# Splitting the copied columns 62 to 66 between ScalarE and VectorE, and copying 108 groups at other rates

## The chip, the cores and the metric

The kernel runs on one core of a Trainium2 chip. The metric is the time of one execution on the device in microseconds (us); the median of several runs is given. The engines are named as the profile names them: PE (TensorE, matmul) and PEld (its weight loads), DVE (VectorE), ACT (ScalarE), POOL (GpSimd), SP (SyncE, which issues DMAs).

## The reference

One layer of message passing on a graph of 12500 nodes with 64 features and 200000 edges with 32 features. The edges come sorted by destination.

```
msg_in    = concat(nodes[src], nodes[dst], edge_features)        # 200000 x 160
messages  = relu(msg_in @ mW1 + mb1) @ mW2 + mb2                 # 160 -> 128 -> 64
agg       = segment_sum(messages, dst, 12500)
upd       = relu(concat(nodes, agg) @ uW1 + ub1) @ uW2 + ub2
out       = layernorm(nodes + upd)
```

## The kernel before

The product of the source node's features with its rows of mW1 is computed once per node: a table `tab_a` of 12500 rows of 128 numbers, in device memory, and likewise `tab_b` for the destinations. Then the edges are worked off in 261 groups of 6 tiles of 128 edges (the last group has 3 tiles), one group to a step `s` of a long unrolled loop. For a group:

- POOL gathers the source rows of `tab_a` with one indirect DMA per tile (L223, into `xg`). It may run up to some nine groups ahead; a group's buffer comes free when its rows have been added.
- PE (`edge_part(s)`, L385) multiplies the edges' features and a one-hot selection of the destination's rows into a PSUM tile `pc`. It is issued one step ahead.
- DVE (`node_part(s)`, L408) adds the gathered rows to `pc`; ACT (L409) takes the ReLU into `h`.
- PE (`collect(s)`, L441 and L444) sums `h` by destination, one step later. The messages' second layer is applied after the sum.
- About every ten steps at first, and every four at the end, a stretch of nodes is complete and is updated, normalised and stored (`close`, `update`, `activated`, `residual`, `squares`, `statistics`, `deviation`, `norm`, `store`).

Some groups are **copied groups** (the list `COPIED`). Of such a group, POOL gathers 4 tiles instead of 6. For the other two tiles the features of the source nodes are copied, one column of 128 numbers per pair of edges (one edge of each tile), out of a transposed copy of the nodes that lies on chip (`xtop` has the features in the upper half of its partitions and zeros below, `xbot` the other way round). A copy adds or ORs a column of the one and a column of the other into a column of `xc`. A copied group has 128 such columns. PE then multiplies `xc` by the weights (L388, four matmuls of a copied group, with accumulation into `pc`).

The columns are shared out by `ACTS`: columns 0 to ACTS - 1 of a copied group are copied by ACT (`singly`, an ACTIVATE with the other column as bias, L358), the rest by DVE (`joined`, a bitwise OR, L365). `portion(s, total)` gives the columns that are due in step `s`: `PACE` is a list of (first step, copied groups per step), `progress(s)` is its sum up to `s`, and of the j-th copied group the share `progress(s - 1) - j` to `progress(s) - j` is copied in step `s`. The j-th copied group is the one three steps after the step in which `progress` reaches j + 1, so that its columns are there when PE wants them; groups from 258 on are never copied.

The addresses of the columns are values in registers of the copying engine. `addresses` (L334) loads them with one register load for up to `CHUNK` = 8 columns of one copied group (two addresses a column).

`share` cuts a step's columns into parts, for the places where they are issued, and the parts into portions of up to 8 columns. DVE's columns of a step go into three parts in an even step and into two in an odd one, all parts but the last of a whole number of 8 columns. DVE's order in an even step: add (L408), first part, comparison of the next 12 tiles' destinations (`select`, L257), second part, `sel` (L263), last part. In an odd step: add, first part, last part. Work of the updates stands between. ACT's columns of a step are issued at its end, in one part (`singly(s, 0, 1)`): ReLU, work of the updates, all the columns, next ReLU.

Of the kernel before, what the change touches and what calls it, by code (L numbers as in the profile page):

```python
# [70 lines left out]
U8 = mybir.dt.uint8  # L71
YBASE = XBASE + 4 * XCOLS
LEAD = 8
PACE = ((11, 0.435), (50, 0.458), (130, 0.438), (170, 0.425), (261, 0))
FINAL = 258


def progress(s):

    return sum(r * max(0, min(s + 1, b) - a) for (a, r), (b, _) in zip(PACE, PACE[1:]))  # L80

# [3 lines left out]
    while progress(s) >= len(COPIED) + 1 and s + 3 < FINAL:  # L85
        COPIED.append(s + 3)
LAST = 4 * (N - 1)
ACTS, CHUNK = 64, 8


def updates():
# [934 lines left out]
```

## Time and profile before

| | |
|---|---|
| median of 3 runs | 1726.23 us (1725.64 to 1727.5) |
| the profiled execution | 1724.81 us, its span 1723.0 us |
| mean granted clock of TensorE | 0.582 |
| busy: PE, DVE, ACT, POOL | 84%, 62%, 90%, 74% of the span |
| gathers (L223) | 1289 from `tab_a`, 60 from `in_x` |
| column copies | 6848 on ACT (L358), 6848 on DVE (L365) |
| register loads for them (L334) | 1006 on ACT, 1037 on DVE |

The profile is of one execution. Busy time counts what an engine's datapath does; the load of a register or the issue of a DMA is not counted. "Idle before" is the time in which an engine did nothing ahead of an instruction, with what ended it; "issue" means that nothing in the profile held it up, which includes the engine's own sequencer loading registers or preparing a DMA.

### The profile page before, as it was taken

The numbers are of one execution on the slowest core, as the hardware profiler recorded it, in microseconds if no ns is written. First come the engines' busy times: TensorE is split into PE (matmuls) and PEld (weight loads), VectorE is DVE, ScalarE is ACT, GpSimd is POOL, SyncE is SP. The second block draws the span as 40 slices with busy tenths as digits, with TensorE's granted clock in tenths as the row PEclk, the third lists the DMA queues.
The fourth block names the chain that finished last, engine by engine and source line by source line (L and its number), as shares of the span: only waits on it lengthen the run. The fifth ranks groups of instructions, "written<-read, shape, count | busy, mean of one in ns | idle before, by whom it ended". The sixth has DMA issues, their size and how long they took to land. (4 is left out here: it accounts for less than half of the span.)

```text
span 1723.0 us, 47177 instructions
## 1 busy us (share of the span) xinstructions
PE 1444.9 (84%) x9576; PEld 1251.9 (73%) x9608; DVE 1062.7 (62%) x7605; ACT 1555.2 (90%) x7279; POOL 1277.0 (74%) x1358
## 2 busy tenths in 40 slices
PE   2696888888878888888888988888887898999987
PEld 2585777787767777777776887776776677877776
DVE  1426666666666666666666666666666666666563
ACT  0176999999999999999999999999999999999892
POOL 7777777777777777777777777777777777777771
PEclk8575555556555555655565555556666656555576
DMA  8783433433333333333333333343333443334332
GB/s 208 202 182 99 118 109 111 125 101 93 94 95 97 92 101 94 98 102 96 105 98 108 108 109 106 104 112 110 108 104 107 112 111 109 110 107 111 105 108 63
DMA packets 205695, 190.92 MB, mean 111 GB/s; under 512 B 55938, under 2 KB 171862, under 8 KB 205414
## 3 DMA queue, kind: packets, MB, share of 16 engines
q1 hardware_dynamic: 147700, 92.42, 19.6%
q0 software_dynamic: 43168, 86.53, 18.4%
q10 hardware_dynamic: 14546, 8.93, 1.9%
q8 instruction: 91, 1.49, 0.3%
q14 instruction: 190, 1.55, 0.3%
HBM read 170.26 MB, written 17.47 MB: 109 GB/s over the span
## 5 line engine op out<-in xcount | busy, mean ns | idle before, releaser
L223 POOL DMA_INDIRECT xg<-tab_a,src_s x1289 | 1218.4, 945 | 393.1 <-issue 356.1
L358 ACT ACTIVATE xc<-xtop,xbot 128x1 f32 x6848 | 1299.2, 290 | 31.3 <-issue 21.4
L365 DVE TENSOR_TENSOR xc<-xtop,xbot 128x1 int32 x6848 | 584.7, 153 | 451.3 <-issue 440.2
L444 PE MATMUL sums<-sel,h 128*128 128x32 f32 x3126 | 642.9, 372 | 79.3 <-ACT h L409 78.4
L444 PEld LDWEIGHTS sums<-sel,h 128*128 128x128 f32 x3126 | 609.2, 296 | 104.4 <-ACT h L409 89.5
L385 PE MATMUL pc<-rhs,l 64*128 64x128 f32 x3126 | 421.0, 412 | 81.5 <-DVE tb L610 28.8
L385 PEld LDWEIGHTS pc<-rhs,l 64*128 64x128 f32 x3126 | 348.1, 289 | 145.4 <-issue 63.0
L408 DVE TENSOR_TENSOR pc<-pc,xg 128x768 f32<-128x768 f32 (+1 forms) x250 | 212.9, 852 | 76.9 <-PE pc L385 26.7
L409 ACT ACTIVATE h<-pc 128x768 f32<-128x768 f32 x250 | 200.3, 801 | 25.4 <-DVE pc L408 24.5
L257 DVE TENSOR_TENSOR l<-l,cps 128x768 f32<-128x768 int32 (+1 forms) x134 | 126.7, 945 | 28.9 <-DMA l<-in_dst_row 17.5
L441 PEld LDWEIGHTS <-one 128*1 128x1 bf16 x1563 | 57.6, 83 | 84.9 <-issue 74.8
L441 PE MATMUL cnt<-sel,one 128*1 128x32 bf16 x1563 | 94.3, 187 | 0.7 <-issue 0.5
L388 PE MATMUL pc<-w1a,xc 64*128 64x128 f32 x428 | 80.5, 384 | 0.0
L263 DVE TENSOR_TENSOR sel<-cps,drc 128x384 f32<-128x384 f32 x131 | 71.3, 545 | 12.6 <-PE sums L444 12.5
L223 POOL DMA_INDIRECT xg<-in_x,src_s x60 | 57.6, 959 | 19.1 <-issue 18.0
L388 PEld LDWEIGHTS pc<-w1a,xc 64*128 64x128 f32 x428 | 71.5, 298 | 0.0
L482 PE MATMUL pu<-xw,uz 128*128 128x480 f32 (+2 forms) x64 | 61.9, 1071 | 0.3 <-DVE xw L459 0.3
L602 ACT COPY tb<-pb 128x512 f32<-128x512 f32 (+1 forms) x13 | 7.4, 569 | 60.1 <-DMA tab_a<-tb 21.1
L439 PE MATMUL cnt<-zero_b 128*1 128x512 bf16 x32 | 18.5, 578 | 47.1 <-DVE xw L459 42.5
L483 PE MATMUL pu<-sums_s,w2u 128*128 128x480 f32 (+2 forms) x64 | 54.4, 952 | 0.0
L498 PE MATMUL cps<-ux,xw 128*128 128x64 f32 x244 | 45.7, 348 | 8.5 <-DVE sel L263 7.9
L498 PEld LDWEIGHTS cps<-ux,xw 128*128 128x128 f32 x244 | 41.0, 253 | 13.8 <-DVE sel L263 10.3
(111 smaller groups left out, 598.6 us busy)
## 6 DMA issues: line engine op xcount, KB each, us to landing
l<-in_dst_row SPq DMA_DIRECT2D x262, 96.0 KB
l<-in_eT SPq DMA_DIRECT2D x262, 96.0 KB
xg<-tab_a,src_s POOLq DMA_INDIRECT x1289
rhs<-tab_b SPq DMA_DIRECT2D x361, 32.0 KB
tab_b<-tb SPq DMA_DIRECT2D x13, 512.0 KB
rhs<-tab_b SPq DMA_DIRECT2D x387, 16.0 KB
tab_a<-tb ACTq DMA_DIRECT2D x12, 512.0 KB
out<-y SPq DMA_DIRECT2D x30, 128.0 KB
```

Of the source, the lines that this page charges most:

```text
L223: nc.gpsimd.indirect_dma_start(out=a[:, i, :] if s < XG else a[:, i // 2, i % 2, :], out_offset=None, in_=A[:, :] if s >= XG else x[:, :], ...
L257: nc.vector.tensor_tensor(l[r], l[r].bitcast(I32), node[r].unsqueeze(2).broadcast_to([r.stop - r.start, SUP // 2, P]), op=ALU.is_equal)
L263: nc.vector.tensor_tensor(s[:, :nt], slot.unsqueeze(1).broadcast_to([P, nt, WIN]), drc[:, g * SUP:g * SUP + nt].unsqueeze(2).broadcast_to( ...
L358: nc.scalar.activation(o[:, e:e + 1], top.bitcast(F32), AF.Identity, bias=bot.bitcast(F32))
L365: nc.vector.tensor_tensor(o[:, e:e + 1].bitcast(I32), top.bitcast(I32), bot.bitcast(I32), op=ALU.bitwise_or)
L385: nc.tensor.matmul(pc[:, b, k, :], L[g][q:q + 64, m, :], rhs[g % 2][q:q + 64, w, :], start=s >= XG or k == 0, stop=s >= XG and not copied)
L388: nc.tensor.matmul(pc[:, b, k, :], xc[s][q:q + 64], w1a[q:q + 64], start=False, stop=True)
L408: nc.vector.tensor_tensor(pc[:, :, :m], pc[:, :, :m], a[:, :, :m], op=ALU.add)
L409: nc.scalar.activation(h, pc, AF.Relu)
L441: nc.tensor.matmul(pn[:, bass.ds(ws[i], WIN)], one, SB[g][:, k0 + i, :, 1], start=False, stop=ends and i == n - 1)
L444: nc.tensor.matmul(ps[:, bass.ds(ws[i], WIN)], h[:, i % 2, i // 2, :], S[g][:, k0 + i, :], start=False, stop=ends and i == n - 1)
L498: nc.tensor.matmul(py[:, i], xw[u % 2][:, i * P:(i + 1) * P], ux, start=i == 0, stop=False)
```

## The change

ACT copies the first 62 columns of a copied group, DVE the other 66. The four rates of `PACE` rise by 2.6%, 2.2%, 0.6% and 0.7%; the list of copied groups that follows from them has 108 entries, not 107, and 75 of the 107 groups of before are replaced by a neighbour (one to four steps earlier for the same place in the list). Nothing else is changed.

```
-PACE = ((11, 0.435), (50, 0.458), (130, 0.438), (170, 0.425), (261, 0))
+PACE = ((11, 0.4465), (50, 0.468), (130, 0.4405), (170, 0.428), (261, 0))
...
-ACTS, CHUNK = 64, 8
+ACTS, CHUNK = 62, 8
```

## The prediction

> **What bounds the kernel now.** The page first: its span, and the busy share of each engine.
>
> ```profile
> span 1723.0 us, 47177 instructions
> PE 1444.9 (84%) x9576; PEld 1251.9 (73%) x9608; DVE 1062.7 (62%) x7605; ACT 1555.2 (90%) x7279; POOL 1277.0 (74%) x1358
> ```
>
> The groups name the work that the change touches: the gathers, and the copies on the two engines.
>
> ```profile
> L223 POOL DMA_INDIRECT xg<-tab_a,src_s x1289 | 1218.4, 945 | 393.1 <-issue 356.1
> L358 ACT ACTIVATE xc<-xtop,xbot 128x1 f32 x6848 | 1299.2, 290 | 31.3 <-issue 21.4
> L365 DVE TENSOR_TENSOR xc<-xtop,xbot 128x1 int32 x6848 | 584.7, 153 | 451.3 <-issue 440.2
> ```
>
> POOL's 74% is an artefact of what counts as busy: a gather takes 945 ns, and nearly all of the idle time before gathers is "issue" (393.1 / 1289 = 0.305 us each). So POOL gathers without a pause, every 1.25 us. It is not the bound, though. The timeline at the end shows how far ahead it is:
>
> ```profile
> 1688.95 0.94 POOL L223 DMA_INDIRECT xg<-tab_a,src_s  x1 [0.30 <-issue]
> ...
> 1703.06 0.97 DVE L408 TENSOR_TENSOR pc<-pc,xg 128x768 f32<-128x768 f32 x1
> ```
>
> The row at 1703.06 adds the rows of group 259. Those were gathered three gathers before the last one, so by 1688.95 - 3 x 1.25 + 0.94 = 1686.1: 17 us earlier. What uses the gathers is the late side, and the time is the sum of its steps. If it were never late, about 17 us could be had and no more.
>
> The busy time by stretch shows who holds up the steps. I cut the trace close to where the rate of the copies changes (steps 50, 130, 170) and at step 236, where the updates come about every fourth step; the second fence has the ReLUs, one to a step, of the first three stretches.
>
> ```profile
> core 0: us, PE busy (x) PEld busy (x) DVE busy (x) ACT busy (x) POOL busy (x), PEclk, DMA share, GB/s
> 121.00:384.00 263.00, 214.82 (x1451) 196.00 (x1451) 173.09 (x1206) 235.46 (x1112) 198.99 (x211) 0.51 0.40 111
> 384.00:890.00 506.00, 425.31 (x2725) 374.49 (x2730) 328.28 (x2531) 503.31 (x2457) 382.55 (x406) 0.54 0.34 97
> 890.00:1140.00 250.00, 222.92 (x1387) 192.91 (x1391) 163.62 (x1228) 246.74 (x1185) 189.03 (x201) 0.55 0.38 107
> 1140.00:1554.00 414.00, 360.78 (x2393) 303.66 (x2404) 271.22 (x1975) 402.83 (x1915) 312.77 (x332) 0.62 0.40 109
> 1554.00:1690.00 136.00, 121.96 (x784) 100.62 (x787) 82.06 (x566) 119.34 (x553) 102.94 (x109) 0.61 0.39 107
> ```
>
> ```profile
> L409 ACT ACTIVATE h<-pc x40: 782/788/811, 122.3 to 380.6; 128x768 f32<-128x768 f32 x40
> L409 ACT ACTIVATE h<-pc x80: 782/807/889, 387.0 to 886.1; 128x768 f32<-128x768 f32 x80
> L409 ACT ACTIVATE h<-pc x40: 783/792/810, 892.4 to 1135.7; 128x768 f32<-128x768 f32 x40
> ```
>
> Call the five stretches A to E. ACT is busy 99.5% of B and 98.7% of C. DVE seems to have a third of its time free, but that is the trap of this case. The waits, for A to E in order, say how much of the free time stands before a column copy with the cause "issue":
>
> ```profile
> DVE xc L365 <- issue: 65.7, 118, 1.6
> ...
> DVE xc L365 <- issue: 161.3, 309, 1.4
> ...
> DVE xc L365 <- issue: 71.8, 147, 1.1
> ...
> DVE xc L365 <- issue: 110.8, 222, 1.1
> ...
> DVE xc L365 <- issue: 30.7, 59, 1.0
> ```
>
> The timeline of one step in B, with ACT's copies of the same time, shows what that is:
>
> ```profile
> 707.43 0.51 DVE L365 TENSOR_TENSOR xc<-xtop,xbot 128x1 int32 x6 [0.56 <-issue]
> 707.86 0.69 DVE L408 TENSOR_TENSOR pc<-pc,xg 128x512 f32<-128x512 f32 x1
> 709.05 0.68 DVE L365 TENSOR_TENSOR xc<-xtop,xbot 128x1 int32 x8 [0.50 <-issue]
> 710.51 0.68 DVE L365 TENSOR_TENSOR xc<-xtop,xbot 128x1 int32 x8 [0.78 <-issue]
> ...
> 712.98 0.43 DVE L365 TENSOR_TENSOR xc<-xtop,xbot 128x1 int32 x4 [0.32 <-issue]
> 713.41 0.97 DVE L408 TENSOR_TENSOR pc<-pc,xg 128x768 f32<-128x768 f32 x1
> ```
>
> ```profile
> 709.78 5.30 ACT L358 ACTIVATE xc<-xtop,xbot 128x1 f32 x28 [0.23 <-issue]
> ```
>
> ```profile
> L334 DVEq TENSOR_LOAD <-col_a x1037: 342/1102/2403, 124.3 to 1679.9; - x173
> ```
>
> Before each portion of up to 8 columns the engine loads two addresses a column into registers. ACT hides that load behind its slow copies (28 in 5.30 us, 0.19 us each, no gap between); DVE copies 8 columns in 0.65 us and then stands still until the addresses are there. So its "issue" time is work, and DVE's occupation is busy plus issue: 489.6 of 506 us in B (96.8%), 235.4 of 250 in C, 382.0 of 414 in D, 112.8 of 136 in E, 238.8 of 263 in A. ACT and DVE are both nearly full. For ACT and DVE waiting on others in B I read:
>
> ```profile
> DVE pc L408 <- PE pc L388: 3.3, 3, 1.8
> DVE pc L408 <- PE pc L385: 2.8, 2, 1.9
> ...
> ACT h L409 <- DVE pc L408: 0.8, 2, 0.5
> ```
>
> Neither waits for the other to speak of: the bound is ACT by a hair, DVE is next.
>
> **The change, part by part.** Counting the lists of columns step by step, as the rates and the two shares give them, the copies of ACT change by -6, -24, -30, -42 and -50 in A to E, together -152 (6848 to 6696); those of DVE by +64, +126, +40, +70 and -20, together +280 (6848 to 7128). The last stretch loses on both because the last copied group is finished about a step and a half earlier.
>
> *ACT.* Each copy gone is 0.188 us (5.30 / 28): -1, -4.5, -5.6, -7.9 and -9.4 us, -28.6 in all. Its loads go from 1006 to 998 and are hidden either way.
>
> *DVE.* The number of loads hardly changes (1037 to 1038); they become wider, because the added columns nearly all fall into the last, unfilled portion of a step, between other copies and the next add (L408). One column more costs there: a copy, 0.07 us ((0.65 - 0.51) / 2), and a longer load. By the gaps that is 0.115 us (0.78 before 8 columns, 0.32 before 4), by the load's own time 0.127 (from 342 ns, the shortest, 2 columns, to the median 1102 ns, 8 columns). I take 0.19 us a column; the bounds are 0.07, if some other instruction covers the load, and 0.20. So +12.2, +23.9, +7.6, +13.3 and -3.8 us, +53 in all: more than ACT gives back.
>
> One rule speaks against charging the load at all. The Trainium skill (DMA: Bandwidth & Descriptors, section Latency and other measured facts) puts a tensor_load at a floor of about 600 ns that unrolling spreads; with a flat load a wider portion would be free but for its copies, and DVE would pay 280 x 0.07 = 20 us. The trace disagrees on both counts: 342 ns at the narrow end, and 1102 ns for most. The sum goes by the trace; the rule's case is the first rival.
>
> *What a stretch then takes.* I compare the new occupation with the old length.
> - A: DVE 251.0 of 263, ACT 234.4. It still fits, but this stretch is mixed with the table's and the weights' work on PE and DVE, and there is little between the add and the ReLU. Half of the 12 us: +5 (0 to +12).
> - B: DVE 489.6 + 23.9 = 513.5 us, over the old 506; ACT 498.8. DVE becomes the bound. 513.5 is the least; of the 16.4 us that were neither busy nor issue some half stays: 520, +14 (+4 to +24).
> - C: DVE 243.0, ACT 241.1, of 250. Each now nearly as full as the fuller one was: -1 (-3 to +3).
> - D: DVE 395.3, ACT 394.9, of 414. The fuller engine was at 97.3%; with both equal a little less well packed: -5 (-8 to 0).
> - E: ACT 109.9, DVE 109.0, of 136, but PE is busy 122 and has the chain of the updates: -3 (-9 to 0).
>
> *POOL.* One more copied group is two gathers less, -2.5 us, on the engine that is 17 us ahead: nothing. A DVE that is later frees the gathered rows later, and POOL may pause in B; it can afford that.
> *PE.* Four more small matmuls; nothing. That groups are copied on other steps moves no wait of SP's queue.
>
> Sum: +5 + 14 - 1 - 5 - 3 = +10 us. The profiled execution took 1724.81 us (span 1723.0), the median is 1726.23 (1725.64 to 1727.5), so the same +10 on the median gives 1736 us. A difference under 0.2% (3.5 us) I take as no change.
>
> **The rivals.**
> *The wider loads are free (faster).* If the sequencer fetches addresses early enough, or the load is flat as that page has it, a column costs DVE 0.07: B becomes 498.4 for DVE against 498.8 for ACT, and ACT's relief shows: about 0 in A, -3 in B, -5 in C, -7 in D, -4 in E, -19, and the gathers stop it at about -17: 1709 us. For it: DVE's add is done before ACT's ReLU asks in B (ACT waits 0.8 us in all), so some lateness is swallowed. Against: 309 gaps of 0.52 us on average in B. It decides below 0.1 us a column. Chance 0.23; a part of the effect, ending between 1709 and 1722, lies in this too.
>
> *The halves cancel (no change).* DVE's loss in A and B, some +12, is given back by ACT's relief in C, D and E, where DVE has 15, 32 and 23 us to spare, and ACT's -23 us arrives by half. 1726, chance 0.11.
>
> *The two engines couple (much slower).* With both over 97% in every stretch, each ReLU waits for a late add, PE waits for the ReLU, and the next add for PE; then B takes its +24, A +12, C +3, and D and E return nothing: 1765 at the extreme, 1750 with two thirds of it. Against: the same feedback exists now and costs ACT 0.8 us in B. Chance 0.15, of the slower side.
>
> That the change does not do what it says (108 groups, 62 and 66 columns) I give 1 in 100, within the case of no change: the counts follow from the lists.
>
> **How the numbers follow.** Forecast (slower by 4 to 20 us) 0.51, coupled 0.15, cancelled 0.11, faster 0.23. Faster 0.23, same 0.11, slower 0.66. The upper end, 1750, leaves out about 0.08; the lower end, 1712, leaves out the full gain of the first rival, about 0.1. 1736 is the likeliest.
>
> **What would show it.** Right: 6696 copies at L358, 7128 at L365, 1287 gathers from tab_a; DVE's issue time before copies up from 440 to about 470 us; ACT busy down by some 28 us from 1555; ACT's ReLU (L409) waiting for DVE's add (L408) far more than before, above all between 384 and 900 us, and ACT below 98% there; the 80 ReLUs of B spread over some 514 us, not 499; C to E no longer than before. Wrong: B no longer than before with ACT still at 99%, which would mean that DVE had hidden room; or gains in C and D of more than ACT's copies are worth.

## The result, and the profile after

The changed kernel takes 1754.84 us (median of 6 runs, 1749.64 to 1757.24), the one before in the same measurements 1726.87 us (6 runs, 1724.6 to 1730.07): ratio 1.0158, 95% interval [1.0141, 1.0175]. It is slower, as forecast, but by 28 us and not by 10; 1754.84 lies above the range's end of 1750. The profiled execution of the changed kernel took 1749.64 us, the quickest of its six, so its trace shows 24.8 of the 28 us (1749.64 - 1724.81).

The page of the changed kernel, the lines that answer to those of before:

```profile
span 1747.7 us, 47341 instructions
PE 1459.5 (84%) x9612; PEld 1251.2 (72%) x9612; DVE 1082.4 (62%) x7885; ACT 1538.3 (88%) x7127; POOL 1274.9 (73%) x1356
...
L223 POOL DMA_INDIRECT xg<-tab_a,src_s x1287 | 1216.1, 945 | 403.0 <-issue 363.8
L358 ACT ACTIVATE xc<-xtop,xbot 128x1 f32 x6696 | 1270.4, 282 | 43.4 <-issue 32.5
L365 DVE TENSOR_TENSOR xc<-xtop,xbot 128x1 int32 x7128 | 606.5, 154 | 487.6 <-issue 476.8
```

The counts are as forecast: 6696, 7128 and 1287. DVE's idle time before its copies ("issue") rose from 440.2 to 476.8 us, where about 470 was named, and its copies' busy time from 584.7 to 606.5 us. ACT's copies fell by 28.8 us of busy time; ACT's whole busy time fell by 16.9 us (1555.2 to 1538.3), where 28 was named. DVE's share of the span still reads 62%, as before.

The busy time by stretch, cut at the same steps as before (columns as there; A to E from top to bottom):

```profile
121.00:392.00 271.00, 215.45 (x1436) 195.93 (x1436) 178.88 (x1275) 237.29 (x1121) 204.87 (x218) 0.51 0.42 110
392.00:913.00 521.00, 429.95 (x2750) 373.96 (x2751) 336.56 (x2658) 505.24 (x2430) 386.76 (x410) 0.55 0.36 95
913.00:1163.00 250.00, 221.37 (x1377) 189.50 (x1376) 165.58 (x1266) 241.81 (x1155) 188.38 (x200) 0.56 0.40 107
1163.00:1583.00 420.00, 372.43 (x2402) 309.27 (x2402) 276.63 (x2045) 395.37 (x1864) 317.41 (x336) 0.60 0.41 108
1583.00:1718.00 135.00, 125.63 (x813) 100.88 (x812) 82.46 (x551) 110.29 (x501) 86.85 (x92) 0.63 0.39 103
```

The table has each stretch from the start of its first ReLU (steps 10, 50, 130, 170, 236) to that of the next, and step 257 as the end of E, read from the ReLUs' rows and compared with the profile before. The runs of the experiments are in it too.

| us against before | A | B | C | D | E |
|---|---|---|---|---|---|
| forecast | +5 | +14 | -1 | -5 | -3 |
| the change | +6.2 | +15.6 | 0.0 | **+7.7** | -6.6 |
| split62: the split alone | +3.3 | +9.3 | -1.2 | +10.2 | +2.7 |
| rates_only: the rates alone | +4.3 | +9.5 | -1.0 | +3.8 | -7.1 |
| from170: the change from step 170 on | -1.5 | +1.6 | -0.8 | +9.1 | -6.8 |
| even_less: DVE's columns shifted from step 170 on | +5.5 | +16.5 | +0.9 | +4.5 | -9.6 |
| split66: the opposite split | -3.7 | +10.1 | +1.3 | +3.9 | -0.1 |
| changed_noload: no loads on DVE | -13.8 | -7.9 | -9.6 | +11.3 | -6.4 |
| lower105: 105 copied groups | -4.9 | -4.6 | -4.5 | +6.8 | -4.4 |

from170 runs A to C as the kernel before does: its -1.5, +1.6 and -0.8 are the least that one execution varies by. Each row is of one execution, and those of one kernel lie further apart as a whole: 10 us for split62 and from170, 14 for rates_only, 19 for split66. The traced one was 3.9 us above the median of its runs for split62 and 5.2 below it for rates_only; so a number of 3 or 4 us in a single row is weak evidence. The only stretch that went clearly against its forecast is D. Two rows, before and after, have its 66 ReLUs from the first to the last, 406.8 and 414.8 us:

```profile
L409 ACT ACTIVATE h<-pc x66: 782/793/843, 1142.3 to 1549.1; 128x768 f32<-128x768 f32 x66
```

```profile
L409 ACT ACTIVATE h<-pc x66: 782/792/811, 1163.0 to 1577.8; 128x768 f32<-128x768 f32 x66
```

### The profile page after: what moved, and what is told of

It reads as the page before. It is cut to its first block, busy times and chain, and to the rows that moved or that the text cites. A ratio compares the mean times of both kernels' runs of the same rounds, so it can differ in the third digit from the quotient of the medians.

```text
span 1747.7 us, 47341 instructions
## 1 busy us (share of the span) xinstructions
PE 1459.5 (84%) x9612; PEld 1251.2 (72%) x9612; DVE 1082.4 (62%) x7885; ACT 1538.3 (88%) x7127; POOL 1274.9 (73%) x1356
## 5 line engine op out<-in xcount | busy, mean ns | idle before, releaser
L358 ACT ACTIVATE xc<-xtop,xbot 128x1 f32 x6696 | 1270.4, 282 | 43.4 <-issue 32.5
L365 DVE TENSOR_TENSOR xc<-xtop,xbot 128x1 int32 x7128 | 606.5, 154 | 487.6 <-issue 476.8
L409 ACT ACTIVATE h<-pc 128x768 f32<-128x768 f32 x250 | 199.3, 797 | 55.2 <-DVE pc L408 53.3
L408 DVE TENSOR_TENSOR pc<-pc,xg 128x768 f32<-128x768 f32 (+1 forms) x250 | 212.5, 850 | 50.4 <-PE pc L385 17.1
L257 DVE TENSOR_TENSOR l<-l,cps 128x768 f32<-128x768 int32 (+1 forms) x134 | 126.6, 945 | 28.2 <-DMA l<-in_dst_row 19.3
L263 DVE TENSOR_TENSOR sel<-cps,drc 128x384 f32<-128x384 f32 x131 | 71.5, 546 | 7.7 <-PE sums L444 7.5
```

The costliest lines, as they stand in the source:

```text
L257: nc.vector.tensor_tensor(l[r], l[r].bitcast(I32), node[r].unsqueeze(2).broadcast_to([r.stop - r.start, SUP // 2, P]), op=ALU.is_equal)
L263: nc.vector.tensor_tensor(s[:, :nt], slot.unsqueeze(1).broadcast_to([P, nt, WIN]), drc[:, g * SUP:g * SUP + nt].unsqueeze(2).broadcast_to( ...
L358: nc.scalar.activation(o[:, e:e + 1], top.bitcast(F32), AF.Identity, bias=bot.bitcast(F32))
L365: nc.vector.tensor_tensor(o[:, e:e + 1].bitcast(I32), top.bitcast(I32), bot.bitcast(I32), op=ALU.bitwise_or)
L408: nc.vector.tensor_tensor(pc[:, :, :m], pc[:, :, :m], a[:, :, :m], op=ALU.add)
L409: nc.scalar.activation(h, pc, AF.Relu)
```

## The experiments

The ratios are to the kernel before on the same chip.

### DVE without register loads (changed_noload)

```
 def addresses(k, a, m, engine):
+    if engine == ET.DVE:
+        return [(e, x8[:, 4 * e:4 * e + 4], y8[:, 4 * e:4 * e + 4]) for e in range(a, m)]
```

> The changed kernel without DVE's register loads: DVE copies fixed columns instead of those of the edges' source nodes (that part of the result is left out); ACT's copies and everything else stay. Theory 1 (DVE's loads are what fills it): DVE has some 250 us more room, ACT's relief of 28.6 us shows, to the reserve of 17: 1710 us, 1% faster than before. If the cost lay in the copies themselves or in PE: 1745 or more.

Measured: 1706.44 us, ratio 0.9873 [0.9842, 0.9905]. The group of DVE's copies (L368 in this kernel) has no idle time left before it, where the changed kernel has 487.6 us:

```profile
L368 DVE TENSOR_TENSOR xc<-xtop,xbot 128x1 int32<-128x1 int32 x7128 | 553.1, 150 | 0.0
```

DVE copies fixed columns here, so the kernel leaves out the columns of DVE's source nodes; the number of copies is the same. The same 7128 copies, without their loads, turn 28 us lost into 20 us gained. So DVE's "issue" time is occupation, and the change makes more of it (440.2 to 476.8 us). What the 280 added copies cost by themselves is not shown: all loads are gone here, not only what the change added to them, and the kernel before was not run without loads at this speed. Stretch A, which lost 6.2 us in the changed kernel, now gains 13.8: there DVE had set the pace even before. From D on this kernel waits for gathers, which is why its D is 11.3 us longer (waits of D, and the last gather of the timeline):

```profile
DVE pc L411 <- DMA xg<-tab_a,src_s: 103.8, 39, 5.3
```

```profile
1685.35 0.94 POOL L223 DMA_INDIRECT xg<-tab_a,src_s  x1 [0.30 <-issue]
```

Its span is 1705.1 us, so from the last gather's start to the end are 19.7 us; in the kernel before 34.0 (1723.0 - 1688.95). That leaves 14 us as the reserve of the gathers, not 17, and two gathers fewer add 2.5.

### Each part of the change alone (split62, rates_only)

```
-ACTS, CHUNK = 64, 8        +ACTS, CHUNK = 62, 8                                    split62
-PACE = ((11, 0.435), ...   +PACE = ((11, 0.4465), (50, 0.468), (130, 0.4405), ...  rates_only
```

> One part of the change alone: ACT 62 and DVE 66 columns, with the old rates and 107 copied groups. ACT copies 214 columns fewer, DVE 214 more. Theory 1 (DVE's occupation, 0.19 us a column): DVE +6.5, +13.7, +6.8, +10.6, +3.0 us in A to E, so DVE is full in B and B takes about +6, the rest about +2: 0.5% slower than before. Theory 2 (nearly equal engines pack badly): both are nearly equal in D as well, D takes +5 or more: 0.8 to 1.1% slower. Theory 3 (the extra copied group and the higher rates are what costs): ACT's relief of 40 us shows up to the reserve of 17 us: 1% faster.

> The other part of the change alone: the new rates and 108 copied groups, with 64 columns for each engine. Both engines copy 64 columns more: +30, +50, +6, +14, -36 in A to E. If each stretch follows the copies that are added to ACT, the fuller engine: +5.6, +9.4, +1.1, +2.6, -6 us, +12 us, 0.7% slower, and together with the split alone (0.79%) the 1.58% of the change. If the split is all of it: no change. If the parts multiply (each alone harmless): under 0.4%.

Measured: split62 1741.78 us, 1.0079 [1.0052, 1.0105]; rates_only 1735.64 us, 1.0087 [1.0055, 1.0119]. The two halves add up as a whole (0.79% + 0.87%, and 1.58% together); in D the single executions do not (10.2 + 3.8 us, and 7.7 together). split62's 0.79% is at the lower end of theory 2 (0.8 to 1.1%), theory 1's 0.5% lies just outside the interval, and D went theory 2's way; theory 3, that ACT's relief would show, is out. In rates_only B is 9.5 us longer, for 9.4 us of copies added to ACT. D is 10.2 us longer with the split alone, although ACT has 54 copies less there.

### The change from step 170 on (from170)

```
+def acts(j):
+    return 62 if j >= 72 else 64
-PACE = (..., (170, 0.425), (261, 0))
+PACE = (..., (170, 0.428), (261, 0))
```

> The change from step 170 on alone: groups whose columns are copied from then on go 62 to ACT and 66 to DVE, at the rate of 0.428 (107 copied groups); before step 170 all as before. In the changed kernel D was 7.7 us longer, where 5 less was forecast. Theory D1 (DVE's free time in D is not usable: in the steps that matter its add was just in time before already): D is 7 us or more longer here too, E 0 to -3, 0.3 to 0.5% slower. Theory D2 (D is longer in the changed kernel because of what goes before, such as its larger lateness): D is 0 to 5 us shorter, E too, 0.3% faster.

Measured: 1730.0 us, 1.0024 [1.0009, 1.0040]. D is 9.1 us longer with nothing changed before it, E 6.8 us shorter. D2 is out: the loss arises in D itself. The waits of D, before and in from170 (L414 and L415 are its add and its ReLU):

```profile
ACT h L409 <- DVE pc L408: 2.2, 6, 0.6
```

```profile
ACT h L415 <- DVE pc L414: 12.3, 20, 1.3
```

ACT's ReLU waited six times for DVE's add, now 20 times. In the changed kernel it is 12.6 us, 19 times. In the changed kernel the granted clock of TensorE in D was 0.60, where the kernel before had 0.62 (third column from the end). Here it is 0.62 and D is longer all the same, so the clock is not needed for the loss:

```profile
1142.00:1564.00 422.00, 359.88 (x2397) 303.08 (x2408) 276.79 (x2043) 397.07 (x1867) 318.96 (x339) 0.62 0.39 108
```

### Two columns from even to odd steps (even_less)

```
+late = lambda s: 2 * (s % 2 == 0 and s >= 170)
 ... int(((progress(s + d) - j) * total - late(s + d)) / 2 + 1e-6) * 2      # DVE's columns only
```

> The changed kernel with DVE's columns shifted from step 170 on: two fewer in each even step, two more in each odd one, the same in all. In the changed kernel the ReLUs that follow an even step's work on DVE (with the comparison of the next tiles and sel in it) came 6.52 us after the one before in D, the others 6.24. Theory P (what DVE has in the even steps decides in D; its free time lies in the odd ones, where it cannot be used): D back from 421 to about 414 us, 1.1% slower than before instead of 1.6%. If the place does not matter: D at 421, 1.6% slower. If DVE simply is full in D: the same.

Measured: 1748.2 us, 1.0115 [1.0080, 1.0149], against 1.0158 [1.0141, 1.0175] for the change; the intervals overlap a little. D is 3.2 us shorter than in the changed kernel and E 3.0, where 7 were expected in D, and the ReLU's wait for the add fell from 12.6 to 8.5 us:

```profile
ACT h L410 <- DVE pc L409: 8.5, 14, 1.2
```

The direction is theory P's, the size is half, and not far from what one execution varies by. So the place of DVE's work seems to matter in D, but it is not shown to be the whole cause; the part on why the prediction was wrong has the steps themselves.

### The opposite split (split66)

```
-ACTS, CHUNK = 64, 8
+ACTS, CHUNK = 66, 8
```

> The opposite split: ACT 66 and DVE 62 columns, old rates, 107 copied groups. ACT copies 214 more: +6.4, +13.5, +6.8, +10.5, +3.0 us in A to E; DVE is relieved of as many. If ACT alone sets the time wherever DVE has room: B +13, C +6, D +8, A and E +2 each, 1.8% slower. If in D the two hand the bound to each other from step to step, what DVE gains there gives back half: D +3 to +5, B +13, C +5: 1.4% slower. If DVE were the bound before: faster.

Measured: 1733.39 us, 1.0040 [1.0016, 1.0065], less than either of the two slower cases. B is 10.1 us longer (13 expected, ACT has 13.5 us more). D is 3.9 us longer for 10.5 us more on ACT, the number that was expected of two engines that hand the bound to each other. Its trace shows something simpler there: ACT is busy 409.87 of 417 us (98%), and its ReLU hardly waits for the add.

```profile
1149.00:1566.00 417.00, 383.03 (x2403) 319.91 (x2403) 267.96 (x1920) 409.87 (x1966) 315.46 (x334) 0.58 0.39 109
```

```profile
ACT h L409 <- DVE pc L408: 1.3, 3, 0.9
```

So in D of this kernel ACT is the bound, which it is not with 62 columns. A is 3.7 us *shorter*: with DVE as the bound there, as changed_noload has it, that fits, and the expectation, which had ACT cost 2 us there, was wrong. In B and D the even split of before is between two worse ones: B +9.3, 0, +10.1 and D +10.2, 0, +3.9 for 62, 64 and 66 columns on ACT.

### Fewer copied groups (lower105)

```
-PACE = ((11, 0.435), (50, 0.458), (130, 0.438), (170, 0.425), (261, 0))
+PACE = ((11, 0.4285), (50, 0.4511), (130, 0.4314), (170, 0.4186), (261, 0))
```

> 64 and 64 columns, all rates lower by 1.5%: 105 copied groups instead of 107. Both engines copy 128 columns fewer (3.0, 6.8, 3.4, 4.9 and 6.0 us of ACT in A to E, about the same of DVE); POOL has four gathers more, 5 us. If ACT and DVE are the bound in B and just in time in the others, and POOL's 17 us are a reserve: the stretches lose those amounts, POOL ends at 1695 us and the tail after it was some 17 us in the kernel without loads: 1713 us, 0.7% faster. If D's length comes from something else than the copies (PE and the updates), D stays at 413 and it is 0.4% faster. If the copies were no bound: no change or slower by POOL's 5 us.

Measured: 1712.4 us, 0.9914 [0.9888, 0.9940]: faster than both kernels. A, B and C lose 4.9, 4.6 and 4.5 us. D is 6.8 us longer. In its last part the gathers have become the late side, as they had without loads: from the end of a group's last gather on POOL to the start of its add there are 2.6 us in the last 26 steps of D (median), 2.3 us in changed_noload, and 17.8 in the kernel before. Whether that is all of the 6.8 us is not shown. The end is 19.4 us after the start of the last gather, as in changed_noload (the span is 1713.6 us):

```profile
1694.19 0.94 POOL L223 DMA_INDIRECT xg<-tab_a,src_s  x1 [0.30 <-issue]
```

So it cannot tell what sets D when gathers are early, which is what it was run for; it does show that the kernel before copied too much, and the change more still.

### Runs that do not tell

Eleven more runs, all but two of them of kernels or parts above, fell on three chips on which the kernel before itself takes 2473 to 2489 us, so they say nothing about this change. The waits of acts62 (the same kernel as split62) show that something else holds it up there:

```profile
DVE xc L365 <- issue: 723.9, 1196, 2.2
POOL xg L223 <- DVE pc L408: 657.8, 169, 18.8
...
ACT xc L358 <- issue: 333.8, 559, 2.1
```

DVE and ACT stand longer before copies than in split62 (466.1 and 42.0 us there), and the profile knows no reason; POOL waits for DVE, which it hardly does above. The register loads themselves take no longer (median 1102 ns on DVE, 1104 in split62). What holds these chips up stays open. The ratios there: acts62 0.9993 [0.9956, 1.0029], pace108 (as rates_only) 1.0000 [0.9963, 1.0038], after_noload (as changed_noload) 0.9880 [0.9827, 0.9932], acts66 (as split66) 1.0041 [1.0019, 1.0064], late_only and late_half (as from170) 0.9928 [0.9889, 0.9966] and 0.9946 [0.9920, 0.9972], fewer105, copies105 and groups105 (as lower105) 1.0082 [1.0051, 1.0112], 1.0058 [1.0022, 1.0094] and 1.0043 [1.0011, 1.0074]. The change from step 170 on, which loses at 1727 us, gains here, and 105 groups, which gain there, lose here; the opposite split and the kernel without loads come out alike on both. None is evidence for or against a theory of this kernel at 1727 us. Their expectations, in the order of the ratios above:

> One part of the change alone: ACT 62 and DVE 66 columns, with the old rates and 107 copied groups. ACT copies 214 columns fewer, DVE 214 more. Theory 1 (DVE's occupation, 0.19 us a column): DVE +6.5, +13.7, +6.8, +10.6, +3.0 us in A to E, so DVE is full in B (503 us before any wait) and B takes about +6, the rest about +2: 1735 us. Theory 2 (nearly equal engines pack badly): both are nearly equal in D as well, D takes +5 or more: 1740 to 1745. Theory 3 (the extra copied group and the higher rates are what costs, DVE is not full): ACT's relief of 40 us shows up to the reserve of 17 us: 1710 us.

> The other part alone: the new rates and 108 copied groups, with 64 columns for each engine. Both engines copy 64 columns more: +30, +50, +6, +14, -36 in A to E. Theory 1: ACT +9.4 us in B, where it was 99.5% full, +2 in A, +1 in C, +3 in D, -4 in E: 1737 us. Theory 2: the same or a little more. Theory 3: nearly all of the 28 us, 1750 us.

> The changed kernel without DVE's register loads: DVE copies fixed columns instead of those of the edges' source nodes (that part of the result is left out); ACT's copies and everything else stay. Theory 1 (DVE's loads are what fills it): DVE has some 250 us more room, ACT's relief of 28.6 us shows, to the reserve of 17: 1710 us. If the cost lay in the copies themselves or in PE: 1745 or more.

> The opposite split: ACT 66 and DVE 62 columns, old rates, 107 copied groups. ACT copies 214 more: +6.4, +13.5, +6.8, +10.5, +3.0 us in A to E. If ACT alone sets the time (DVE has hidden room): +40 us, 2.3% slower. Theory 1 (the fuller of the two decides, DVE next behind ACT): B to 517 us, C to 255, D to 415 to 418, A and E +2 each: 1.4 to 1.7% slower. If the two were equally to blame everywhere, what DVE gains gives half of it back: under 1%.

> The change from step 170 on alone: groups whose columns are copied from then on go 62 to ACT and 66 to DVE, at the rate of 0.428 (107 copied groups); before step 170 all as before. In the changed kernel D was 7.7 us longer, where 5 less was forecast. Theory D1 (DVE's free time in D is not usable: in the steps that matter its add was just in time before already): D is 7 us or more longer here too, E 0 to -3, 0.3 to 0.5% slower. Theory D2 (D is longer in the changed kernel because of what goes before, such as its larger lateness): D is 0 to 5 us shorter, E too, 0.3% faster.

> The change from step 170 on alone: groups whose columns are copied from then on go 62 to ACT and 66 to DVE, at the rate of 0.428 (107 copied groups); before step 170 all as before. In the changed kernel D was 7.7 us longer, where 5 less was forecast. Theory D1 (DVE's free time in D is not usable: in the steps that matter its add was just in time before already): D is 7 us or more longer here too, E 0 to -3, 0.3 to 0.5% slower. Theory D2 (D is longer in the changed kernel because of what goes before, such as its larger lateness): D is 0 to 5 us shorter, E too, 0.3% faster.

> 64 and 64 columns, all rates lower by 1.5%: 105 copied groups instead of 107. Both engines copy 128 columns fewer; POOL has four gathers more, 5 us. The reserve of POOL (17 us before) is spent where the engines are full: ACT and DVE have some 20 us less each, POOL ends at 1695 us instead of 1690, the tail after it was 17 us at the least in the kernel without loads: 1713 us, 0.7% faster. If the copies were no bound: 1726 or more.

> 64 and 64 columns, all rates lower by 1.5%: 105 copied groups instead of 107. Both engines copy 128 columns fewer; POOL has four gathers more, 5 us. The reserve of POOL (17 us before) is spent where the engines are full: ACT and DVE have some 20 us less each, POOL ends at 1695 us instead of 1690, the tail after it was 17 us at the least in the kernel without loads: 1713 us, 0.7% faster. If the copies were no bound: 1726 or more.

> 64 and 64 columns, all rates lower by 1.5%: 105 copied groups instead of 107. Both engines copy 128 columns fewer (3.0, 6.8, 3.4, 4.9 and 6.0 us of ACT in A to E, about the same of DVE); POOL has four gathers more, 5 us. If ACT and DVE are the bound in B and just in time in the others, and POOL's 17 us are a reserve: the stretches lose those amounts, POOL ends at 1695 us and the tail after it was some 17 us in the kernel without loads: 1713 us, 0.7% faster. If D's length comes from something else than the copies (PE and the updates), D stays at 413 and it is 0.4% faster. If the copies were no bound: no change or slower by POOL's 5 us.

Two kernels ran nowhere else. before_noload, the kernel before without DVE's loads, gave 0.9991 [0.9964, 1.0018]:

> The kernel before without DVE's register loads, with the same part left out. Theory 1 (ACT is the bound by a hair): B stays at 503 to 506 us, stretches A, C and D lose what they waited for DVE, 2 to 8 us each: 1715 us. Theory 2 (two nearly equal engines lose by their alternation): the same 1715, with ACT above 99% in C and D too. If ACT alone set the time: 1726, no change.

early_only, the change up to step 170 alone, gave 1.0035 [1.0011, 1.0058]:

> The complement: the change up to step 170 alone (62 and 66 columns, rates 0.4465, 0.468, 0.4405), from then on 64 and 64 at 0.425; 108 copied groups. A +6, B +15, C 0 as in the changed kernel. Theory D1: D as before, E -3 to -6: 1.0 to 1.2% slower. Theory D2: D 7 us longer as in the changed kernel: 1.5% slower.

## Why the prediction was right or wrong

**The bound: right.** That DVE's issue time is work, that the loads make it, and that the change asks more of DVE than it gives ACT back: changed_noload bears out the first two, and split62 and rates_only show that each half of the change costs by itself. The rule of the Trainium skill that was weighed there (DMA: Bandwidth & Descriptors, section Latency and other measured facts) is a tensor_load floor of about 600 ns; the prediction read it as a flat cost, which would have had the wider loads free. DVE's issue time grew by 36.6 us with as many loads as before (1037 and 1038), so that did not hold, and the rival built on it fell.

**A, B and C: right.** Forecast +5, +14, -1, measured +6.2, +15.6, 0.0; the 80 ReLUs of B lie over 514.7 us (392.1 to 906.8), where 514 was named. That half of DVE's added time would show in A, and that half of B's slack would stay, were estimates which no run bears out; that they came so close is in part luck. The price of a column held too: in B, DVE's busy and issue time went from 489.6 to 512.5 us (336.56 and 175.9), +22.9 where the sum had +23.9:

```profile
DVE xc L365 <- issue: 175.9, 306, 1.2
...
POOL xg L223 <- DVE pc L408: 15.7, 22, 1.4
...
ACT xc L358 <- issue: 8.7, 28, 0.6
...
ACT h L409 <- DVE pc L408: 4.8, 10, 0.8
```

These are waits of B in the changed kernel. POOL pauses for buffers, as forecast, at no cost. The sign that was named for B came only in part: ACT's ReLU waits 4.8 us for the add (0.8 before), and 7.1 us more are lost before ACT's copies (8.7 us in 28 gaps; 1.6 us in 6 before). A late add seems to leave ACT's own loads unhidden too; no run separated that.

**D: wrong, by 12.7 us.** The step that failed is the last one of the part on the stretches: "The fuller engine was at 97.3%; with both equal a little less well packed: -5 (-8 to 0)." The occupations came within 3 us (DVE 276.6 + 121.6 = 398.2 where 395.3 was forecast, ACT 395.4 where it was 394.9); what failed is that the fuller of two sums decides how long a stretch takes. Both sums are 5 to 6% short of its 420 us. The runs showed in its place that the stretch is made step by step, and that even and odd steps differ. In an even step DVE also compares destinations (L257 and L263). The times from one ReLU of D to the next, added up by the step of the first (33 of each kind), and the ReLU's waits for the add, all from the traces' rows of L408 and L409 (other line numbers in from170 and even_less):

| us in D | after an even step | after an odd step | ReLU waits for the add, odd steps |
|---|---|---|---|
| before | 205.5 | 207.5 | 1.9 (5 times) |
| the change | **215.0** | 205.7 | **11.8** (17) |
| split62 | 216.9 | 206.3 | 11.2 (15) |
| from170 | 214.9 | 207.2 | 11.1 (17) |
| even_less | 210.4 | 207.1 | 6.0 (9) |
| split66 | 207.9 | 209.1 | 1.3 (3) |

The whole loss of D, +9.5 and -1.8 us, lies after the even steps, where the add comes late for the ReLU of the odd step that follows. Before 15 of the 19 ReLUs that wait in the changed kernel (10.6 of the 12.6 us) the add had followed DVE's own work without a gap worth the name (0.14 us at most): DVE was full in that step. Yet over the whole stretch it stands idle for some 22 us. The loss arises in D itself (from170) and comes with the split to 62 (split62); with 66 columns on ACT this wait is nearly gone, and D's +3.9 there goes with an ACT that is busy for 98% of it. The free time of DVE before, 32 us by that sum, could not be used where it was needed. What is left open is why two columns fewer in the even steps took away only about half of their loss (215.0 to 210.4 us); PE and the updates may have a part in it, and lower105, which was to tell, ran into the gathers.

The third rival had the mechanism, waits of the ReLU for a late add, and 1750 us at a chance of 0.15. It put the extra loss into A and B (+12 and +24; they came at +6.2 and +15.6) and let D return nothing, where D lost 7.7. Its premise, both engines over 97% in every stretch, does not follow from the prediction's own sums: A has DVE at 95% and ACT at 89%, D has both at 95%.

**E: right in sign,** -6.6 where -3 was forecast. That the copies end earlier is enough for that: from170 and rates_only have it too, split62 has not.

**The rest.** The start and the end of the execution add 2 us that the sum did not have. The median lies 5.2 us above the profiled run, where the kernel before had 1.4 at the time of the forecast; no trace shows those. With D at its measured +7.7 the sum would have been +23, 1749 us: D's term is the largest part of the miss, the 2 us and the changed kernel's higher median are the rest.

**The rivals.** "The wider loads are free" is out (split62, changed_noload). "The halves cancel" is out: D gave nothing back. The reserve of the gathers, which would have limited a gain, was 14 us and not 17.

## What to carry to other kernels

An engine that loads addresses before short instructions is as full as its busy time and its unexplained gaps before those instructions together, whatever its share of the span reads. Where two engines are nearly equally full and wait for each other once a step, taking work from the one and giving it to the other can lose in either direction, as it did here, and a stretch takes longer than the larger of the two sums. Where steps differ in kind, add up each kind by itself, and count the steps in which one engine is just in time, not the free time. And look first at who ends early: here the gathers had 14 us to spare, so the change to make was to copy less.

## What the runs showed of the hardware that was not expected

A register load's time goes by its width. Each load on DVE in the kernel before, paired with the copies that used it, took 0.35 us for 2 columns, 0.61 for 4, 0.87 for 6 and 1.12 for 8 (medians of 90, 169, 92 and 669 loads): 0.13 us a column. In the changed kernel all loads on DVE together take 1024.9 us, where they took 989.1, with one load more, and DVE's gaps before copies are 36.6 us longer.

On three of the nine chips that the experiments met, the unchanged kernel took 2473 to 2489 us instead of 1727, with longer gaps before instructions and no reason in the profile; which kernel is the faster one was not always the same there.
